# A two-layer graph network on one core: eight node tiles by counts instead of seven, and x's halves kept in DRAM

## The chip, the cores and the metric

The kernel runs on one core of one Trainium2 chip. The metric is the device time of one execution in microseconds. Before the change it is 1335.6 us, the median of three runs (1334.89 to 1339.82).

## What is computed

x has 6250 rows (nodes) of 256 values; src and dst name 100000 edges, sorted by dst. dst is 6250 times the square of a uniform number, so low nodes have many edges and high nodes few. The network adds to each node the rows of its edges' sources, twice, with two dense layers behind each sum, and the result is added to x and normalized:

```python
def gin_agg(h, src, dst, eps, n):
    agg = segment_sum(h[src], dst, num_segments=n)
    return (1.0 + eps) * h + agg
h = gin_agg(x, src, dst, eps1, n)      # 6250 x 256
h = relu(h @ W1a + b1a)                # 256 -> 512
h = relu(h @ W1b + b1b)                # 512 -> 512, this is h1
h = gin_agg(h, src, dst, eps2, n)      # 6250 x 512
h = relu(h @ W2a + b2a)                # 512 -> 512
out = layernorm(x + (h @ W2b + b2b))   # 512 -> 256
```

## The kernel before, in words

**Tiles and chunks.** Nodes are cut into 49 tiles of 128, edges into 782 chunks of 128. The sums are formed in two ways.

**Sums by gathers.** For the chunks of the higher nodes, POOL issues one indirect DMA per chunk (line 461), which fetches 128 source rows into a piece of the buffer `early` (in layer 2 also `late`). PE multiplies four such chunks with selection matrices (line 954), a second matmul puts the group's rows in their places (line 1001), and DVE adds them to the accumulators of the tiles which the group can reach (line 1011). Six pieces of four chunks can be under way; a piece's buffer comes free with its sum.

**Sums by counts.** For the lowest tiles, `HEAVY` of them, the kernel counts in layer 1 how often each source appears for each node, and multiplies these counts with all of x or h1. Counting takes one chunk after the other: DVE makes two comparison matrices (`ca`, line 1523, and `cb`, line 1532), PE multiplies them (line 1571), and DVE adds the result to the table `at` at a place that the data give (line 1594). `at` is a ring of `RING` = 4 tiles, so at most four tiles' counts are in it, and counting of further tiles waits until those of an earlier pass are cleared (line 1437). A step takes 1, 2, 4 or 8 chunks; it works from the highest heavy tile down.

**Passes of layer 1.** The heavy tiles are taken two at a time: with seven, the passes are (6,5), (4,3), (2,1) and (0). In each pass all of x goes by in 13 ranges of up to four tiles. `loading` fetches a range into `raw` (line 1188, on SP's queue), `halving` splits it into an upper half of few bits and the rest, side by side in `xh` (ACT at lines 1385 and 1392, DVE at line 1394), `factoring` turns counts into the factors `cf` (ACT, line 1415), stores them as uint16 for layer 2 (line 1423 and a DMA on ACT's queue) and has them cleared where the ring is used again, and `multiplying` forms the products (line 1457), 128x512 per node tile and source tile, so both halves in one matmul. At a pass's end `adding` puts them into the accumulators (line 1472).

**Layer 2.** h1 is read in 13 ranges from the last to the first, split in the same way (lines 1220 to 1225), the stored counts are loaded and converted (lines 1243 and 1255), and for each range and each heavy tile PE forms two products per source tile, one for each half (line 1331, 128x512). DVE collects them (line 1274). x's or h1's own rows are added as seeds (lines 866 and 883 for most tiles, 1302 and 1311 for the heavy ones of layer 2).

**Dense layers.** When a block of one or two tiles has all its parts, `dense` transposes it (line 1047), multiplies with the first weights (line 1086) and the second (line 1115), and stores h1 (line 1128) or normalizes and stores the output.

**What sets the order.** All instructions are issued in an order that a small planner works out when the program is built. It keeps a clock, costs for each operation, priorities for PE, DVE and ACT (sums by gathers first, then merges and counting, then dense work, and the products of layer 2 last), and due times for DMAs (`LOAD`, `LANDINGS`, `COUNTS` and the like). On the chip each engine and each queue then works in that fixed order. The second layer's gathers read h1 and so wait until all of it is stored.

Of the kernel before, what the change touches and what calls it, by code (L numbers as in the profile page):

```python
# [21 lines left out]
SLOTS = 32  # L22
BURST = 4
PIECES = 6
HEAVY = (7, 7)
RING = 4
W = 10
RANGE = 4
# [133 lines left out]
GATHERS = (1.28, 1.265)  # L162
LANDINGS = (5.0, 6.0)
LOAD = 6.0
SEEDS = (6.0, 12.0)
WHOLE = 16.0
COUNTS = 12.0
# [169 lines left out]
def tile_gin_residual_layernorm(  # L337
# [415 lines left out]
    def ordered(ctx):  # L753
# [4 lines left out]
        ctx.enter_context(tc.manual_schedule())  # L758

        ranges = [range(k, min(k + RANGE, NT)) for k in range(0, NT, RANGE)]  # L760
        counts = odram.tile([len(ranges), HEAVY[1], P, RANGE * P], mybir.dt.uint16, name="counts")

        def layer(number, ctx, table, width, scale, weights, ba, wide):
# [408 lines left out]
            def whole_rows(ks):  # L1172

                return min(len(ks), N // P - ks[0])
# [181 lines left out]
                    cleared[ts].more(sum(t >= RING for t in ts) * len(ranges))  # L1356

            def first_products():
                xh_room = Tiles(loan, [P, RANGE, 2, width], F32R, "xh", 2)
                raw_room = Tiles(loan, [P, RANGE, width], F32, "raw", 2)  # L1360
                ci_room = Tiles(loan, [P, RANGE * P], mybir.dt.uint16, "ci", 2)
                xh_of = {}
                turns = [(ts, r) for ts in PASSES for r in range(len(ranges))]
# [1 line left out]
                made = {(t, r): Event(plan) for ts, r in turns for t in ts}  # L1365
                factors = {}

                def loading():
                    yield ("rest", 80.0)
                    for ts, r in turns:  # L1370
                        raw = yield ("get", raw_room, 0)
                        in_rows(ranges[r], raw.tile, table)
                        token = yield ("get", xh_room, 0)
                        xh_of[ts, r] = token
                        plan.start(halving(ts, r, token.tile, raw))

                def halving(ts, r, xh, raw):
                    ks = ranges[r]
                    yield ("rest", LOAD)
                    n = whole_rows(ks)  # L1380
                    for m, js in ((P, slice(0, n)), (rows(NT - 1), slice(n, len(ks)))):
                        if js.start < js.stop:
                            c = (js.stop - js.start) * width
                            yield ("on", "ACT", act(c), 1)
                            nc.scalar.copy(xh[:m, js, 0, :], raw.tile[:m, js, :])
                            for j in range(js.start, js.stop, 2):
                                two = slice(j, min(j + 2, js.stop))
                                token = yield ("get", banks, 2)
                                c = (two.stop - j) * width
                                yield ("on", "ACT", act(c), 1)  # L1390
                                ap = bank[token.number][:m, :c].rearrange("p (k d) -> p k d", d=width)
                                nc.scalar.copy(ap, raw.tile[:m, two, :])
                                yield ("on", "DVE", dve(c), 1)
                                nc.vector.tensor_tensor(  # L1394
                                    xh[:m, two, 1, :], ap, xh[:m, two, 0, :], op=ALU.subtract
                                )
                                token.release()
                    raw.release()
                    plan.then(halved[ts, r].set)

                def factoring():
                    for ts in PASSES:
# [37 lines left out]
                def multiplying():  # L1440
                    for ts in PASSES:
# [3 lines left out]
                        for r, ks in enumerate(ranges):  # L1445
# [7 lines left out]
                            for i, t in enumerate(ts):  # L1453
# [6 lines left out]
                                        start=(k == 0), stop=(k == NT - 1),  # L1460
                                    )
                                factors[t, r].used()
                            xh_of[ts, r].release()
                        for t, token in zip(ts, tokens):
                            plan.then(plan.start, adding(t, token))

# [14 lines left out]
            def counting():  # L1481
# [1 line left out]


                F16 = mybir.dt.float16
                cb_room = Tiles(loan, [P, NT * W], F16, "cb", 10)
                ca_room = Tiles(loan, [P, BATCH, P], F16, "ca", 4)
                yield ("on", "DVE", 2.5, 4)
                si = loan.tile([P, NC], I32, tag="si", name="si")
# [399 lines left out]
```

## Time and profile before

The profiled execution took 1333.73 us, its span is 1332.0 us.

| | busy, us | instructions |
|---|---|---|
| PE, matmuls | 1171.7 | 6027 |
| PE, weight loads | 756.0 | 6027 |
| DVE | 872.8 | 2031 |
| ACT | 603.2 | 1118 |
| POOL | 963.8 | 1002 |

Of the 305.72 MB moved, 194.31 went through the queue of the gathers. Layer 1 lasts until about 676 us, when the first gather of h1 starts; layer 2 fills the rest. In the rows a line number is that of the kernel before, a name such as `early<-h,srcs` gives what is written and from what, "xN" is a count, and behind the last bar stands the idle time of the engine just before these instructions and what ended it. Busy time of PE contains the overlap of pipelined matmuls.

### The profile page before, as it was taken

Reading aid. Unit: us, or ns where it says so; the run is one execution under the profiler, and the core shown is the slowest. Engines: PE = TensorE matmul, PEld = TensorE weight load, DVE = VectorE, ACT = ScalarE, POOL = GpSimd, SP = SyncE. Lnnn points to the kernel's source line nnn. Section 1 sums busy time; section 2 is a strip of 40 time slices with the busy share of each in tenths; the row PEclk is TensorE's granted clock in tenths of the full one; section 3 lists DMA queues with packets and bytes.
Section 4 is the critical chain, followed back from the end, with each engine's and each line's share of the span. In section 5 each row is a group of like instructions: output and inputs, shape, how many; then the busy total and the mean of one; then the engine's idle time right before and its main releaser. Section 6 shows DMA issues by size and latency. Waiting matters only on the chain. (4 is left out here: it accounts for less than half of the span.)

```text
span 1332.0 us, 18717 instructions
## 1 busy us (share of the span) xinstructions
PE 1171.7 (88%) x6027; PEld 756.0 (57%) x6027; DVE 872.8 (66%) x2031; ACT 603.2 (45%) x1118; POOL 963.8 (72%) x1002
## 2 busy tenths in 40 slices
PE   2379888999899999878759899999989999999986
PEld 1145554655454655444436667767667766677755
DVE  7689888697897787323127668777756655653443
ACT  0213677767675763454255354334334433432222
POOL 6877777777777777777457677777777777777770
PEclk8589999999999999968879899999989999999999
DMA  3635666667676775566669889888889999877782
GB/s 103 189 119 178 182 219 198 207 199 227 207 225 188 219 239 170 151 211 193 198 228 333 296 268 310 252 278 287 289 271 309 301 310 301 289 244 240 242 244 69
DMA packets 160860, 305.72 MB, mean 230 GB/s; under 512 B 25672, under 2 KB 93150, under 8 KB 160754
## 3 DMA queue, kind: packets, MB, share of 16 engines
q0 software_dynamic: 63232, 194.31, 47.2%
q1 hardware_dynamic: 75110, 84.23, 19.3%
q10 hardware_dynamic: 22412, 25.89, 5.6%
q8 instruction: 51, 0.84, 0.3%
q14 instruction: 55, 0.45, 0.1%
HBM read 273.90 MB, written 30.44 MB: 228 GB/s over the span
## 5 line engine op out<-in xcount | busy, mean ns | idle before, releaser
L461 POOL DMA_INDIRECT early<-in_x_dram,srcs x494 | 488.9, 990 | 158.9 <-issue 127.4
L461 POOL DMA_INDIRECT early<-h,srcs x250 | 239.8, 959 | 101.4 <-issue 58.8
L461 POOL DMA_INDIRECT late<-h,srcs x244 | 232.5, 953 | 77.6 <-issue 60.2
L1011 DVE SCALAR_TENSOR_TENSOR acc<-bank,mask,acc 128x256 f32<-128x256 f32 (+1 forms) x368 | 212.8, 607 | 39.4 <-PE bank L1001 34.8
L1086 PE MATMUL bank<-zt,w2a_s 128*128 128x256 f32 (+2 forms) x864 | 181.8, 366 | 7.7 <-DVE acc L1011 6.5
L1115 PE MATMUL bank<-w1b_s,ht 128*128 128x512 f32 (+1 forms) x392 | 184.7, 599 | 1.1 <-DVE acc L1011 0.8
L1086 PEld LDWEIGHTS bank<-zt,w2a_s 128*128 128x128 f32 x864 | 154.8, 195 | 30.4 <-DVE acc L1011 6.9
L954 PE MATMUL bank<-early,sel 128*32 128x256 f32 (+1 forms) x1488 | 134.3, 475 | 32.7 <-DMA early<-h,srcs 15.3
L1331 PE MATMUL bank<-upper,cf 128*128 128x512 f32 (+1 forms) x343 | 149.2, 435 | 13.9 <-ACT upper L1220 13.5
L1331 PE MATMUL bank<-xr,cf 128*128 128x512 f32 (+1 forms) x343 | 138.2, 403 | 0.8 <-DVE xr L1225 0.8
L1594 DVE TENSOR_TENSOR at<-bank,at 128x490 f32 x174 | 115.9, 666 | 28.2 <-ACT cf L1415 14.7
L907 DVE TENSOR_TENSOR sel<-iota,slot 128x256 f32<-128x256 f32 (+2 forms) x116 | 50.6, 436 | 123.5 <-PE bank L954 119.5
L1086 PE MATMUL bank<-zt,w1a_s 128*128 128x256 f32 (+2 forms) x432 | 103.2, 389 | 13.7 <-ACT zt L1059 10.4
L1001 PE MATMUL bank<-split,to 128*128 128x256 f32 (+2 forms) x340 | 100.0, 415 | 15.6 <-ACT split L987 8.7
L1115 PEld LDWEIGHTS bank<-w1b_s,ht 128*128 128x128 f32 (+1 forms) x392 | 73.3, 191 | 70.8 <-issue 58.6
L1457 PE MATMUL bank<-xh,cf 128*128 128x512 f32 (+1 forms) x343 | 104.1, 440 | 8.7 <-DVE xh L1394 8.6
L1255 ACT CAST cf<-ci 128x512 fp32r<-128x512 uint16 (+1 forms) x91 | 53.8, 595 | 121.4 <-PE bank L1331 104.3
L1096 ACT ACTIVATE ht<-bank,b2a_s 128x256 f32<-128x256 f32 (+2 forms) x108 | 44.6, 451 | 139.5 <-PE bank L1086 137.0
L954 PEld LDWEIGHTS bank<-early,sel 128*32 128x32 f32 x1488 | 40.0, 112 | 113.4 <-issue 80.2
L1571 PE MATMUL bank<-cb,ca 128*128 128x490 f16 x288 | 87.6, 381 | 16.1 <-DVE at L1594 10.5
L1115 PE MATMUL bank<-w2b_s,ht 128*128 128x256 f32 (+1 forms) x392 | 101.5, 390 | 0.0
L1086 PEld LDWEIGHTS bank<-zt,w1a_s 128*128 128x128 f32 x432 | 81.9, 207 | 32.7 <-ACT zt L1059 14.9
(138 smaller groups left out, 1650.7 us busy)
## 6 DMA issues: line engine op xcount, KB each, us to landing
raw<-in_x_dram SPq DMA_DIRECT2D x48, 512.0 KB, 4.5
h<-h1r ACTq DMA_DIRECT2D x48, 256.0 KB, 2.5
xr<-h SPq DMA_DIRECT2D x12, 1024.0 KB, 7.3
counts<-ci ACTq DMA_DIRECT2D x84, 128.0 KB, 3.4
ci<-counts SPq DMA_DIRECT2D x84, 128.0 KB, 5.0
acc<-h SPq DMA_DIRECT2D x19, 512.0 KB, 7.5
early<-in_x_dram,srcs POOLq DMA_INDIRECT x494
acc<-in_x_dram SPq DMA_DIRECT2D x21, 256.0 KB, 3.9
```

The costliest lines, as they stand in the source:

```text
L461: nc.gpsimd.indirect_dma_start(out=rows_[:, j, :], out_offset=None, in_=table, in_offset=bass.IndirectOffsetOnAxis(ap=srcs[:, c : c + 1], ...
L907: nc.vector.tensor_tensor(sel[:, :n, :], iota[:, :SLOTS].unsqueeze(1).to_broadcast([P, n, SLOTS]), slot[:, c0 : c0 + n].unsqueeze(2).to_br ...
L954: mm = nc.tensor.matmul(pm[b * SLOTS : (b + 1) * SLOTS], sel[:, c - groups[g][0], :], rows_[:, l, :], start=(c == part[0]), stop=(c == par ...
L1001: nc.tensor.matmul(pu[:, i * width : (i + 1) * width], to[:used], split[:used, l, :], start=(once or l == 0), stop=(once or l == 1),)
L1011: nc.vector.scalar_tensor_tensor(acc[t], pu[:, i * width : (i + 1) * width], mask[:, t - lo[g], g : g + 1], acc[t], op0=ALU.mult, op1=ALU.add,
L1086: nc.tensor.matmul(ph[:, (f - o) * TILES * P : (f - o) * TILES * P + nb], wa[:, k, f * P : (f + 1) * P], zt[:, k, :nb], start=(k == 0), st ...
L1115: nc.tensor.matmul(po[:m], ht[:, f, i * P : i * P + m], wb[:, f, :], start=(f == 0), stop=(f == KH - 1),)
L1255: nc.scalar.copy(cf_token.tile[:, :n, :].rearrange("p k j -> p (k j)"), token.tile[:, : n * P],)
L1331: nc.tensor.matmul(bank[token.number][:, :width], cf[:m, j, :], of[:m, j, :], start=(j == 0 and of is upper), stop=(j == len(ks) - 1 and o ...
L1457: nc.tensor.matmul(bank[tokens[i].number][:, : 2 * width], cf[:m, j, :], xh[:m, j, :, :].rearrange("p a d -> p (a d)"), start=(k == 0), st ...
L1571: mm = nc.tensor.matmul(bank[token.number][:, : NT * W], a.tile[:, c % BATCH, :], b.tile, start=(j == 0), stop=(j == n - 1),)
L1594: nc.vector.tensor_tensor(to, bank[token[0].number][:, : NT * W].rearrange("p (k w) -> p k w", w=W), to, op=ALU.add,)
```

## The change

`HEAVY` becomes (8, 8): eight tiles are summed by counts in both layers, and the passes are (7,6), (5,4), (3,2) and (1,0). In layer 1 the halves of x are formed in the first pass alone; each range is then also stored to a DRAM tensor `halves` (`keeping`), and the three other passes load both halves, 1 MB per range, straight into `xh`, without `raw` and without `halving`. `xh` gets three buffers for two, `raw` one for two, and the comparison matrices `cb` eight for ten. `HALVES` is the planner's due time for these DMAs. In the first pass a buffer of `xh` comes free when its products and its store are both done.

```diff
-HEAVY = (7, 7)
+HEAVY = (8, 8)
+HALVES = 9.0
+        halves = odram.tile([len(ranges), P, RANGE, 2, D], F32, name="halves")
             def first_products():
-                xh_room = Tiles(loan, [P, RANGE, 2, width], F32R, "xh", 2)
-                raw_room = Tiles(loan, [P, RANGE, width], F32, "raw", 2)
+                xh_room = Tiles(loan, [P, RANGE, 2, width], F32R, "xh", 3)
+                raw_room = Tiles(loan, [P, RANGE, width], F32, "raw", 1)
...
+                stored = [Event(plan) for _ in ranges]
+
+                def used_rows(r):
+
+                    n, k = whole_rows(ranges[r]), len(ranges[r])
+                    whole = [(slice(0, P), slice(0, n))] if n else []
+                    return whole + ([(slice(0, rows(NT - 1)), slice(n, k))] if n < k else [])
+
                 def loading():
                     yield ("rest", 80.0)
                     for ts, r in turns:
-                        raw = yield ("get", raw_room, 0)
-                        in_rows(ranges[r], raw.tile, table)
-                        token = yield ("get", xh_room, 0)
-                        xh_of[ts, r] = token
-                        plan.start(halving(ts, r, token.tile, raw))
+                        if ts is PASSES[0]:
+                            raw = yield ("get", raw_room, 0)
+                            in_rows(ranges[r], raw.tile, table)
+                            token = yield ("get", xh_room, 0)
+                            xh_of[ts, r] = token
+                            token.users = 2
+                            plan.start(halving(ts, r, token.tile, raw))
+                        else:
+                            yield ("until", stored[r])
+                            token = yield ("get", xh_room, 0)
+                            xh_of[ts, r] = token
+                            for p, js in used_rows(r):
+                                nc.sync.dma_start(token.tile[p, js].bitcast(F32), halves[r, p, js])
+                            plan.at(plan.now + HALVES, halved[ts, r].set)
+
+                def keeping(ts, r):
+                    token = xh_of[ts, r]
+                    for p, js in used_rows(r):
+                        nc.sync.dma_start(halves[r, p, js], token.tile[p, js].bitcast(F32))
+                    yield ("rest", HALVES)
+                    token.used()
+                    yield ("rest", LOAD)
+                    stored[r].set()
...
                     plan.then(halved[ts, r].set)
+                    plan.then(plan.start, keeping(ts, r))
...
-                            xh_of[ts, r].release()
+                            (xh_of[ts, r].used if ts is PASSES[0] else xh_of[ts, r].release)()
...
-                cb_room = Tiles(loan, [P, NT * W], F16, "cb", 10)
+                cb_room = Tiles(loan, [P, NT * W], F16, "cb", 8)
```

## The prediction

> **What bounds the kernel now.** I read the page's busy line first, then the gather rows of its groups, then the timeline of POOL, then busy time by stretches.
>
> ```profile
> PE 1171.7 (88%) x6027; PEld 756.0 (57%) x6027; DVE 872.8 (66%) x2031; ACT 603.2 (45%) x1118; POOL 963.8 (72%) x1002
> ...
> L461 POOL DMA_INDIRECT early<-in_x_dram,srcs x494 | 488.9, 990 | 158.9 <-issue 127.4
> L461 POOL DMA_INDIRECT early<-h,srcs x250 | 239.8, 959 | 101.4 <-issue 58.8
> L461 POOL DMA_INDIRECT late<-h,srcs x244 | 232.5, 953 | 77.6 <-issue 60.2
> ```
> ```profile
> 8.77 1.12 POOL L461 DMA_INDIRECT early<-in_x_dram,srcs  x1 [5.50 <-DVE rawf L534]
> ...
> 650.16 0.95 POOL L461 DMA_INDIRECT early<-in_x_dram,srcs  x1 [0.30 <-issue]
> 676.63 1.13 POOL L461 DMA_INDIRECT early<-h,srcs  x1 [25.53 <-DMA h<-h1r]
> ```
>
> POOL looks 72% busy, but nearly all its idle time is "issue": a gather takes 0.95 us and 0.30 us pass before the next, so POOL can start one every 1.25 us. Layer 1's 494 gathers need 617.5 us at that pace and run from 8.77 to 651.1, 642 us: POOL is at its own pace almost throughout. It then waits 25.53 us for the last rows of h1, and layer 2 begins at 676.63. So layer 1 ends on the gathers plus a tail of 25.5 us.
>
> Layer 2, in stretches (columns: PE busy, weight loads, DVE, ACT, POOL, each with its count, then clock, DMA share, GB/s):
>
> ```profile
> 8.70:651.20 642.50, 540.52 (x2636) 308.08 (x2637) 469.78 (x1124) 342.49 (x612) 488.90 (x494) 0.92 0.63 194
> 676.60:1332.00 655.40, 611.30 (x3296) 436.81 (x3296) 395.19 (x797) 251.53 (x486) 472.30 (x494) 0.97 0.84 271
> 676.60:700.00 23.40, 13.28 (x29) 8.33 (x30) 5.49 (x11) 14.11 (x30) 17.88 (x19) 0.57 0.90 313
> 700.00:750.00 50.00, 43.53 (x218) 30.32 (x218) 35.22 (x60) 22.86 (x42) 37.59 (x40) 0.94 0.94 318
> 750.00:950.00 200.00, 198.62 (x1082) 142.55 (x1081) 155.92 (x311) 83.96 (x159) 149.69 (x157) 1.00 0.87 282
> 950.00:1000.00 50.00, 44.72 (x227) 30.81 (x226) 26.14 (x50) 17.69 (x32) 37.81 (x41) 0.93 0.85 274
> 1000.00:1200.00 200.00, 196.67 (x1077) 140.40 (x1075) 122.80 (x247) 84.60 (x156) 151.55 (x160) 1.00 0.88 293
> 1200.00:1300.00 100.00, 93.09 (x526) 67.24 (x525) 39.61 (x93) 21.64 (x48) 75.88 (x80) 0.99 0.80 241
> ```
>
> POOL keeps its 40 gathers per 50 us here too (160 in 200 us), so gathers pace layer 2 as well; but PE is close behind. Of 655.4 us PE is idle 44.1: 16.6 in the ramp to 750 (23.4 + 50 - 13.28 - 43.53), 16.9 between 750 and 1300 (550 - 533.1), and the remaining 10.6 in the tail. The question is what the one tile more costs PE there.
>
> **The change, layer 1.** From the constants of the plan: chunks by counts go from 288 to 308, so gathers go from 494 to 474 in each layer, groups from 85 to 83, counting steps (L1594) from 174 to 194. POOL loses 20 x 1.25 = 25.0 us in each layer. The other engines:
>
> ```profile
> L1594 DVE TENSOR_TENSOR at<-bank,at 128x490 f32 x174 | 115.9, 666 | 28.2 <-ACT cf L1415 14.7 <-ACT at L1437 7.4 <-PE bank L1571 1.9
> L1532 DVE TENSOR_SCALAR cb<-numbers,spot 128x490 f16<-128x490 f16 x288 | 89.4, 352 | 8.4 <-PE bank L1571 8.3
> L1571 PE MATMUL bank<-cb,ca 128*128 128x490 f16 x288 | 87.6, 381 | 16.1 <-DVE at L1594 10.5 <-DVE cb L1532 4.0 <-DVE xh L1394 1.1
> L1394 DVE TENSOR_TENSOR xh<-bank,xh 128x512 fp32r<-128x512 f32 (+1 forms) x100 | 66.8, 673 | 50.0 <-ACT bank L1392 49.5
> L1392 ACT COPY bank<-raw 128x512 f32<-128x512 f32 (+1 forms) x100 | 57.3, 580 | 20.9 <-DVE at L1594 6.8 <-DVE xh L1394 6.5 <-ACT h1r L1127 3.6
> L1385 ACT CAST xh<-raw 128x1024 fp32r<-128x1024 f32 (+1 forms) x52 | 51.6, 994 | 7.0 <-ACT ci L1423 3.3 <-PE bank L1457 1.2 <-ACT h1r L1127 1.2
> L1415 ACT CAST cf<-at 128x512 fp32r<-128x512 uint16 (+1 forms) x91 | 53.9, 592 | 43.2 <-DVE at L1594 23.3 <-ACT ci L1423 7.2 <-DVE at L1406 2.5
> ```
>
> DVE: 75 of the 100 subtractions of L1394 go (three passes of four), -75 x 0.67 = -50; 20 counting adds (13.3), 20 comparisons (7.0) and some small ones (4) come: -26 us net. ACT: 39 of L1385 and 75 of L1392 go (-38.8 - 43.0); 13 conversions of L1415, 13 copies of L1423 and 13 clearings of L1437, all of the same shape, come at 0.59 us (+23): -58 us. PE: 49 products and 20 counting matmuls come, 80 quick sums go: about +14 us, against 102 us idle in the row of layer 1. None of this is on the gathers' path unless counting becomes late (below). Fewer comparison buffers (8 for 10) can lengthen the 8.3 us for which L1532 waited for L1571; between nothing and as much again, I take nothing.
>
> DMA: x is 6.4 MB, its halves 12.8. Three raw loads go (-19.2), one store and three loads of halves come (+12.8 + 38.4), 20 gathers of 0.13 MB go, 13 count tiles of 0.13 MB come: +31 MB, spread over the some 410 us in which the passes run, so 200 GB/s becomes about 275. Layer 2 runs at 274 to 293 GB/s with POOL at full pace, so the gathers should stand it; hidden. If that cover is gone, a late landing holds PE's next sum and then POOL's buffer.
>
> The new waits sit on SP: a store of halves waits for the subtraction, and a load for a free buffer and a landed store. Behind them on SP queue the seeds of acc and the next raw load. Seeds are asked for well ahead; the raw loads, now with one buffer, are the tighter case, and only pass 1 has them.
>
> Whether the passes stay off the path is read from three places:
>
> ```profile
> 60.00:240.00 180.00, 59.17 (x89) 0.92 0.57 175
> 255.00:552.00 297.00, 56.37 (x85) 0.99 0.67 203
> ```
> ```profile
> 255.00:552.00 297.00, 58.65 (x199) 15.79 (x199) 0.99 0.67 203
> ```
> ```profile
> 255.00:552.00 297.00, 280.67 (x1427) 162.83 (x1426) 239.29 (x561) 179.92 (x321) 226.32 (x233) 0.99 0.67 203
> ```
> ```profile
> 551.66 0.67 DVE L1594 TENSOR_TENSOR at<-bank,at 128x490 f32 x1 [1.86 <-PE bank L1571]
> ...
> 631.68 0.88 DVE L1472 TENSOR_TENSOR acc<-bank,acc 128x256 f32<-128x256 f32 x2 [1.13 <-PE bank L1457]
> ```
>
> The first fence is L1594 alone: 89 steps by 240, then the ring is full and counting waits until pass 1 has been cleared, near 255. The second is L1571 in the rest: 199 chunks in 297 us, 1.49 us each, with DVE 81% and PE 94% busy (third). Counting ends at 552, and the last pass takes 80 us more, to 632. With eight tiles the ring is full after 79 steps, so 229 chunks are left at 255. At the old rate that is 341 us, ending at 596. If DVE set the rate, its 239 us become 239 - 50 + 34 = 223, at 81% 275 us, ending at 530. If PE set it, 281 + 18 = 299 at 94.5% is 316 us, ending at 571. I take 560, the middle of the ends. The last pass then needs no halving: about 13 loads of 1 MB in three buffers. The nearest row is layer 2's load of the same size:
>
> ```profile
> xr<-h SPq DMA_DIRECT2D x12, 1024.0 KB, 7.3
> ```
>
> 13/3 x (7.3 + 2 for the products) = 40 us as the lower end, the old 80 as the upper. I take 55: the last pass ends at 615, before the gathers do (651 - 25 = 626). So layer 1 gives -25. Its ends: -31, if a quarter of the 25 us comes back that the 494 gathers lost against their own pace (642 - 617.5), and, from 596 + 80 = 676 with 23 us behind it, +23.
>
> **Layer 2.** 98 products come (7 x 49 x 2 become 8 x 49 x 2). The page's group gives one a busy time of 0.43 us, but products overlap; the timeline shows what PE really pays:
>
> ```profile
> L1331 PE MATMUL bank<-upper,cf 128*128 128x512 f32 (+1 forms) x343 | 149.2, 435 | 13.9 <-ACT upper L1220 13.5
> ```
> ```profile
> 1005.57 0.39 PE L1331 MATMUL bank<-xr,cf 128*128 128x512 f32 x1
> ...
> 1006.95 0.39 PE L1331 MATMUL bank<-xr,cf 128*128 128x512 f32 x1
> 1007.18 1.08 PE L1001 MATMUL bank<-split,to 128*128 128x512 f32 x4
> ...
> 1016.92 2.78 PE L954 MATMUL bank<-late,sel 128*32 128x512 f32 x24
> 1019.64 1.13 PE L1115 MATMUL bank<-w2b_s,ht 128*128 128x256 f32 x4
> ```
>
> From 1005.57 to 1007.18 there are seven, 0.23 us from start to start, with no gap: 98 x 0.23 = +22.6. The sums of 12 gathers (24 matmuls) take 2.72, so 20 gathers fewer save 4.5; two merges of two matmuls at 0.23 save 0.9. PE's work grows by 17.2 us while POOL's shrinks by 25. POOL alone would let the layer end 25 us sooner, but PE has only 44 us idle: PE becomes the bound. The 16.9 us in the middle are waits that fall away when gathers are always ahead of PE; the ramp and the tail stay. If all of it is filled the layer's length changes by 17.2 - 16.9 = 0, if none by +17; the order is fixed when the program is built and won't fill all, so I take half: +9. ACT (13 casts, 7.7) and DVE (13 adds, 9) have 400 and 260 us free in the layer's row.
>
> **Sum.** 1333.7 (the profiled execution's own time, its span of 1332.0 and 1.7 around it) - 25 + 9 = 1317.7, so **1318**. That execution lies 1.9 under the median of the runs, 1335.6, and 1.2 under their lowest; I don't correct for it.
>
> **A rule that would read this otherwise.** The Trainium skill, "Perfetto Trace Analysis", section "Identifying the Most-Contended Engine", says that matmul busy time is no good measure of PE's headroom, and that the busy share of weight loads should be taken. By that rule PE is 67% loaded in layer 2 (436.81 of 655.4) and not the bound. The time would be that of the first rival. The rows of L1331, 0.23 us from start to start with nothing between, speak for a PE that streams without a gap, and here I follow them.
>
> **The rivals.** (1) POOL paces both layers, because PE's busy row hides room: 1333.7 - 50 = 1284. For it: POOL never drops below 40 per 50 us. Against: the gapless starts. Chance 0.12. (2) The other side: counting, not gathering, ends layer 1. The ring fills ten steps sooner, pass 1 now loads with one raw buffer and holds its halves for the store, and counting goes on at the old 1.49 us per chunk. It decides once the last pass ends later than about 632; past that a microsecond costs a microsecond. With 596 + 65 = 661, and some 23 us for the last two tiles' dense work and its landing, h1 is done at 684, +7, and layer 2's +9 goes on top: 1350. For it: PE is 94% busy just there. Against: DVE loses 50 us of halving. Chance 0.17. (3) Half of layer 1's gain is lost to crowded DMA or that chain, and layer 2 costs +12: 1333.7 - 12.5 + 12 = 1333, no change. Chance 0.13. (4) PE pays in layer 2 what the group's row says, 98 x 0.43 - 5.4 = +37: 1333.7 - 25 + 37 = 1346. For it: the row; against: the starts. Chance 0.06. (5) The change doesn't do what it says: some input's chunk reaches beyond its ten nodes and the general path runs, at a time no row here gives; the widths and margins are the same ones as before, 0.01.
>
> **How the numbers follow.** My forecast has 0.51, and its own range is 1306 to 1328. A change under 0.5% (1329 to 1342) can't be told from none. Faster: 0.12, nearly all of 0.51, and a little of rival 3, 0.64; same: most of rival 3 and the edges, 0.15; slower: rivals 2, 4 and 5 less their edges, 0.21. The range reaches from just above rival 1 to just below rival 2: 1288 to 1348.
>
> **What would show it.** Layer 1: the first gather of h near 651 instead of 676.6, after the last gather of x at 626; the last L1594 near 560, the last pass done by 632. If that pass ends later and PE or ACT waits for halves, rival 2. Layer 2: PE idle below 35 us, gathers below 40 per 50 us with POOL waiting for L954; if POOL keeps its 40 and the last 150 us are shorter, rival 1. Wrong would be above all a first pass that doesn't end by 270.

## The result and the profile after

The kernel after takes 1374.05 us (median of 4 runs, 1366.21 to 1386.56) where the kernel before took 1335.93 beside it: a ratio of 1.031, with a 95% interval of 1.027 to 1.035. It became slower; forecast were 1318 and a range of 1288 to 1348. The profiled execution took 1367.12 us, 7 under the median; its span is 1365.4. Against the profiled execution of before the first layer, counted to the first gather of h, is 14.6 us longer (691.25 for 676.63) and the second 18.8 (674.2 for 655.4).

The gathers' groups and the timeline of POOL, kernel after (busy and mean of one, then the idle time before them and what ended it; in the timeline the start, the duration and in brackets the wait):

```profile
L462 POOL DMA_INDIRECT early<-in_x_dram,srcs x474 | 475.2, 1003 | 150.5 <-issue 123.7 <-PE bank L1600 5.8 <-DVE rawf L535 5.5
L462 POOL DMA_INDIRECT early<-h,srcs x238 | 227.9, 957 | 137.4 <-DMA acc<-h 62.3 <-issue 56.7 <-DMA early<-h,srcs 5.8
```
```profile
627.99 0.95 POOL L462 DMA_INDIRECT early<-in_x_dram,srcs  x1 [0.30 <-issue]
691.25 1.03 POOL L462 DMA_INDIRECT early<-h,srcs  x1 [62.32 <-DMA acc<-h]
1296.04 0.95 POOL L462 DMA_INDIRECT late<-h,srcs  x1 [0.30 <-issue]
```

The last gather of x did come 22 us earlier, near the 25 that the count promised. But POOL then stands for 62 us instead of 25.5: layer 1 no longer ends on its gathers.

**Layer 1.** The whole layer in busy time, before and then after (PE, weight loads, DVE, ACT, POOL, each with its count, then clock, DMA share, GB/s):

```profile
8.70:676.60 667.90, 559.48 (x2729) 318.67 (x2729) 473.42 (x1132) 351.69 (x633) 488.90 (x494) 0.92 0.62 190
```
```profile
8.70:691.20 682.50, 568.98 (x2754) 326.05 (x2754) 447.76 (x1093) 296.61 (x554) 475.20 (x474) 0.95 0.70 231
```

Stretches of the kernel after; first the counting adds alone (L1623, L1594 of before), then two rows of their timeline with nothing of L1623 between them, then the waits of ACT in the last pass, then all engines:

```profile
60.00:210.00 150.00, 52.62 (x79) 0.94 0.65 208
210.00:262.00 52.00, 0.00 (x0) 1.00 0.93 323
262.00:582.00 320.00, 76.86 (x115) 0.98 0.74 243
```
```profile
204.37 1.44 DVE L1623 TENSOR_TENSOR at<-bank,at 128x490 f32 x2
267.13 0.68 DVE L1623 TENSOR_TENSOR at<-bank,at 128x490 f32 x1 [0.57 <-issue]
```
```profile
ACT ci L1452 <- DMA counts<-ci: 18.7, 7, 7.6
```
```profile
262.00:582.00 320.00, 291.16 (x1456) 164.13 (x1456) 236.51 (x567) 131.37 (x249) 244.21 (x247) 0.98 0.74 243
582.00:667.50 85.50, 73.23 (x344) 45.95 (x336) 11.38 (x26) 41.64 (x84) 35.66 (x38) 0.90 0.67 223
667.50:691.20 23.70, 11.24 (x36) 6.42 (x36) 3.55 (x10) 4.45 (x9) 0.00 (x0) 0.87 0.62 195
```

79 steps are counted by 206, then the ring is full, and the adds stand still until 267 (235 to 258 in the kernel before). The other 229 chunks take 320 us from 262 on, 1.40 each, or 1.37 from the first add on: DVE is down to 74% and ACT to 41%, but PE is at 91%. Counting ends at 582. The last pass takes 85 us more, and ACT waits in it for stores of counts to free one of the two `ci` buffers. The last two tiles' dense work and its landing take 23.7 (44 in the kernel before, from 632 to 676.6).

**Layer 2**, in its first 75 us, the stretch to the last gather and the rest; before, then after:

```profile
676.60:751.60 75.00, 58.41 (x251) 40.07 (x252) 41.26 (x71) 36.97 (x72) 55.75 (x58) 0.82 0.93 317
751.60:1301.50 549.90, 533.00 (x2911) 381.09 (x2910) 343.93 (x698) 207.89 (x395) 415.60 (x435) 0.99 0.86 277
1301.50:1332.00 30.50, 19.90 (x139) 15.65 (x137) 10.00 (x28) 6.67 (x19) 0.95 (x1) 0.94 0.17 55
```
```profile
691.20:766.20 75.00, 53.31 (x238) 35.23 (x238) 35.72 (x62) 38.77 (x72) 54.71 (x58) 0.82 0.91 312
766.20:1296.00 529.80, 515.49 (x2769) 366.45 (x2770) 342.84 (x681) 206.51 (x388) 396.49 (x416) 0.99 0.86 279
1296.00:1365.40 69.40, 59.29 (x345) 50.88 (x343) 22.23 (x59) 14.68 (x40) 0.95 (x1) 0.94 0.14 45
691.20:1365.40 674.20, 628.09 (x3350) 452.56 (x3350) 400.79 (x801) 259.95 (x500) 452.14 (x474) 0.97 0.79 259
```

The gathers need 604.8 us (75 + 529.8) for 624.9: 20 fewer, at 1.276 us each where it was 1.265. But behind the last one PE has 59.3 us of work left where it had 19.9, and the stretch grows by 38.9. The groups of that stretch show what it is, before and then after:

```profile
L1115 PE MATMUL bank<-w2b_s,ht 128*128 128x256 f32 x28 | 6.8, 383 | 0.0
```
```profile
L1117 PE MATMUL bank<-w2b_s,ht 128*128 128x256 f32 x72 | 17.6, 381 | 0.0
L1333 PE MATMUL bank<-upper,cf 128*128 128x512 f32 x16 | 6.7, 420 | 0.0
```

A tile needs eight of these matmuls (392 for 49), so nine tiles' second weights lie behind the last gather instead of three and a half, with the last products of the heavy tiles, which in the kernel before were done by 1250.

### The profile page after: what moved, and what is told of

The parts are those of the page before. It is cut to its first block, busy times and chain, and to the rows that moved or that the text cites. A ratio compares the mean times of both kernels' runs of the same rounds, so it can differ in the third digit from the quotient of the medians.

```text
span 1365.4 us, 18905 instructions
## 1 busy us (share of the span) xinstructions
PE 1197.9 (88%) x6106; PEld 779.1 (57%) x6106; DVE 852.7 (62%) x1994; ACT 556.6 (41%) x1054; POOL 929.9 (68%) x962
## 5 line engine op out<-in xcount | busy, mean ns | idle before, releaser
L462 POOL DMA_INDIRECT early<-in_x_dram,srcs x474 | 475.2, 1003 | 150.5 <-issue 123.7
L462 POOL DMA_INDIRECT early<-h,srcs x238 | 227.9, 957 | 137.4 <-DMA acc<-h 62.3
L1333 PE MATMUL bank<-upper,cf 128*128 128x512 f32 (+1 forms) x392 | 169.2, 432 | 24.5 <-ACT upper L1222 23.4
L1623 DVE TENSOR_TENSOR at<-bank,at 128x490 f32 x194 | 129.6, 668 | 62.7 <-ACT cf L1444 45.0
L1333 PE MATMUL bank<-xr,cf 128*128 128x512 f32 (+1 forms) x392 | 157.3, 401 | 0.8 <-DVE xr L1227 0.8
L1486 PE MATMUL bank<-xh,cf 128*128 128x512 f32 x392 | 117.5, 436 | 14.8 <-ACT cf L1444 14.7
L1003 PE MATMUL bank<-split,to 128*128 128x512 f32 (+2 forms) x332 | 96.9, 410 | 14.0 <-ACT split L989 8.6
L1276 DVE TENSOR_TENSOR acc<-bank,acc 128x512 f32<-128x512 f32 x96 | 64.9, 682 | 63.7 <-PE bank L1333 59.1
L1333 PEld LDWEIGHTS bank<-upper,cf 128*128 128x128 f32 (+1 forms) x392 | 75.8, 193 | 47.0 <-ACT upper L1222 24.6
L1486 PEld LDWEIGHTS bank<-xh,cf 128*128 128x128 f32 x392 | 73.3, 194 | 50.2 <-ACT cf L1444 22.7
```

The source lines that it names most:

```text
L462: nc.gpsimd.indirect_dma_start(out=rows_[:, j, :], out_offset=None, in_=table, in_offset=bass.IndirectOffsetOnAxis(ap=srcs[:, c : c + 1], ...
L1003: nc.tensor.matmul(pu[:, i * width : (i + 1) * width], to[:used], split[:used, l, :], start=(once or l == 0), stop=(once or l == 1),)
L1276: nc.vector.tensor_tensor(acc[t], bank[token.number][:, :width], acc[t], op=ALU.add)
L1333: nc.tensor.matmul(bank[token.number][:, :width], cf[:m, j, :], of[:m, j, :], start=(j == 0 and of is upper), stop=(j == len(ks) - 1 and o ...
L1486: nc.tensor.matmul(bank[tokens[i].number][:, : 2 * width], cf[:m, j, :], xh[:m, j, :, :].rearrange("p a d -> p (a d)"), start=(k == 0), st ...
L1623: nc.vector.tensor_tensor(to, bank[token[0].number][:, : NT * W].rearrange("p (k w) -> p k w", w=W), to, op=ALU.add,)
```

## The experiments

These runs went to five chips. On two of them (numbers 11 and 12) the kernel before takes 1334.5 to 1335 us, near the 1335.93 beside the result; on the other three (numbers 2, 3 and 10) it takes 1604 to 1623. They are called the faster and the slower chips here: e1 to e4 and g1 to g4 ran on the faster ones, all others on the slower. Ratios are always to the kernel before on the same chip. In the expectations theory A is rival 2 of the prediction, carried on: the counting chain and the last pass end layer 1, wherever x's halves come from; the theories beside it lay the loss on the halves' traffic and buffers (theory B) or (theory C) on how counting is dealt out to PE.

**Which part costs.** The tiles alone, the halves alone, and both with seven tiles in layer 2:

```diff
-HEAVY = (7, 7)       e1: the kernel before with
+HEAVY = (8, 8)
-HEAVY = (8, 8)       e2: the kernel after with
+HEAVY = (7, 7)
-HEAVY = (8, 8)       e3: the kernel after with
+HEAVY = (8, 7)
```

> The kernel before with eight tiles by counts, x halved anew in every pass (two xh, two raw, ten cb). Theory A, the chain of counting and passes ends layer 1, and eight tiles lengthen it whatever is done with the halves: the table is full after 79 steps instead of 89, pass 1 takes its old 120 us (ends near 258), 229 chunks at the old 1.49 us end counting near 596, the last pass of two tiles takes 85 to 100 us, 23 us follow: first gather of h near 710, 20 us later than with the halves kept; layer 2 as in the changed kernel, 674; time about 1387. Theory B, keeping the halves in DRAM (one raw buffer, stores, 1 MB loads) is what costs layer 1: first gather of h near 655, time about 1331.

> The changed kernel with seven tiles in both layers. Theory A: the full table still stops counting until pass 1 is cleared, some 15 us longer than before, but 199 chunks at 1.40 us end by 550 and the last pass has one tile and no halving, so the gathers end layer 1 as before: first gather of h at 676 to 680, layer 2 655, time 1334 to 1340. Theory B: layer 1 ends about 15 us later, as in the changed kernel: about 1350.

> The changed kernel with eight tiles by counts in layer 1 and seven in layer 2. If the 98 products that PE got in layer 2 are its whole loss there, layer 2 takes 655 us again (674 in the changed kernel) and the time is 1367 - 19 = 1348. If layer 2 is longer because of how it starts (loads and stores of layer 1 in its way), it stays near 670: 1363. Layer 1 should end near 691 as in the changed kernel.

Measured, medians: e1 1365.5 us, ratio 1.024 (1.021 to 1.026); e2 1340.45, 1.004 (1.002 to 1.006); e3 1367.45, 1.025 (1.023 to 1.028). So the tiles cost most, and the halves, which take 75 subtractions from DVE and 114 instructions from ACT, gain nothing by themselves. None of the three fell cleanly on one side of what was expected: e1 ended layer 1 at 695.4 (710 for theory A, 655 for B), e2 at 684.9 (676 to 680, or some 691), and the second layer of e3 took 664.5 (655 if the products were the whole loss, near 670 if the start was). The two layers of e1, of e2, and the second of e3 with its first 75 us:

```profile
8.70:695.40 686.70, 573.13 (x2754) 324.44 (x2754) 493.21 (x1170) 369.00 (x669) 476.42 (x475) 0.93 0.61 183
695.40:1363.00 667.60, 627.56 (x3350) 451.56 (x3350) 401.52 (x802) 259.25 (x500) 452.24 (x474) 0.97 0.80 261
```
```profile
8.70:684.90 676.20, 559.92 (x2729) 321.07 (x2729) 430.52 (x1075) 278.87 (x519) 490.01 (x495) 0.95 0.72 235
684.90:1341.20 656.30, 610.92 (x3296) 435.99 (x3296) 394.92 (x796) 251.56 (x486) 473.11 (x494) 0.97 0.84 271
```
```profile
697.20:1361.70 664.50, 614.67 (x3264) 435.62 (x3264) 394.14 (x796) 252.56 (x483) 471.46 (x494) 0.96 0.83 267
697.20:772.20 75.00, 53.35 (x232) 34.44 (x236) 37.62 (x68) 38.95 (x72) 54.67 (x57) 0.80 0.91 305
```

With eight tiles layer 1 ends at 691 to 695 whether DVE is busy 493 us (e1) or 448 (after). Layer 2 is 12 us longer in e1 too, where x's halves play no part.

In e2 layer 1 still ends on its gathers (POOL stands 20 us behind the last one), but the last one starts at 663.76 for 650.16 before: POOL waited 19.5 us for sums on PE where it had waited 7.2.

```profile
L462 POOL DMA_INDIRECT early<-in_x_dram,srcs x494 | 490.0, 992 | 171.5 <-issue 128.3 <-PE bank L956 19.5 <-DMA early<-in_x_dram,srcs 7.3
```

**The count buffers.** e4 gives the stores of counts four buffers, and takes two from `cb` for the room:

```diff
-ci_room = Tiles(loan, [P, RANGE * P], mybir.dt.uint16, "ci", 2)
+ci_room = Tiles(loan, [P, RANGE * P], mybir.dt.uint16, "ci", 4)
-cb_room = Tiles(loan, [P, NT * W], F16, "cb", 8)
+cb_room = Tiles(loan, [P, NT * W], F16, "cb", 6)
```

> The changed kernel with four ci buffers instead of two (and six cb for eight, for the room). Theory A2: each pass of two tiles is paced by the two buffers out of which the counts are stored, 26 stores at some 3.2 us; then the last pass falls from 85 us to about 55, layer 1 ends 25 to 30 us sooner (near 663), time about 1340. Rival: the loads of halves pace the last pass, which start 6.7 us apart on SP's queue: the last pass stays at 80 to 85 us and the time near 1367 or, through fewer cb, a little above.

Measured: 1370.36 us, 1.028 (1.025 to 1.031). The last pass and what is behind it, kernel e4:

```profile
590.00:656.70 66.70, 51.42 (x254) 31.86 (x254) 7.72 (x19) 34.98 (x65) 40.15 (x43) 0.90 0.77 279
656.70:691.00 34.30, 33.87 (x137) 19.44 (x135) 6.42 (x12) 11.22 (x28) 0.00 (x0) 1.00 0.50 162
```

The pass became 19 us shorter, 66.7 us instead of 85.5, though not down to the 55 that theory A expected. Yet the first gather of h came at 696. Counting ended at 590 instead of 582, PE did 22 us less in the pass (51.42 for 73.23), and after it PE worked almost without a gap for 34 us on dense work that had not been done in it. What the buffers gave was taken back by PE's dense work.

**The counting chain itself.** g1 leaves 58 of the 308 chunks uncounted (steps of more than two chunks count two), so the lowest nodes' sums lack some of their edges:

```diff
-tomake = [c + i for c, n in STEPS for i in range(n)]
+tomake = [c + i for c, n in STEPS for i in range(min(n, 2))]
```

> As f3_fewer_counts: 58 of the 308 chunks are not counted, the lowest nodes' sums lack these edges. On the slower chip the first gather of h came 22 us before that of the changed kernel beside it (816.8 against 838.9). On a chip where the kernel before takes about 1335: if counting and last pass end layer 1, the first gather of h falls from 691 to 651..665, and the ratio to before from 1.03 to about 1.005; if the gathers or the dense work end it, 683 or later.

Measured, two runs: 1351.6 us, 1.013 (1.007 to 1.019). POOL, and PE behind the last pass:

```profile
632.35 0.95 POOL L462 DMA_INDIRECT early<-in_x_dram,srcs  x1 [0.30 <-issue]
676.16 1.10 POOL L462 DMA_INDIRECT early<-h,srcs  x1 [42.86 <-issue]
```
```profile
626.00:676.20 50.20, 42.44 (x181) 23.00 (x179) 10.54 (x22) 15.14 (x33) 5.72 (x7) 0.97 0.42 135
8.70:676.20 667.50, 556.92 (x2696) 321.27 (x2696) 427.40 (x1031) 298.65 (x557) 474.04 (x475) 0.96 0.72 237
```

A miss for theory A in its simple form, which wanted 651 to 665, and no hit for the other side (683 or later). Counting ended at 539 for 582, half of the 81 us that 58 chunks at 1.40 would have given. The chain became 42 us shorter (last pass done at 626 for 667.5), the layer only 15, though the gathers, done by 633, would have let it end some 17 us sooner still (633 and the 25.5 of before; an estimate). The gap is filled by dense work: 42.4 us of PE in the 50.2 behind the pass. PE's busy time in the layer fell by 12.1 us (569.0 to 556.9), the layer by 15.

**How counting is dealt out, and the single raw buffer.** g3 counts up to four chunks per turn of PE instead of two; g4 gives the kernel after its old buffers:

```diff
-for k in range(0, len(todo), 2):           g3
+for k in range(0, len(todo), 4):
-"xh", 3) ... "raw", 1)                      g4
+"xh", 2) ... "raw", 2)
```

> As f2_turn4: up to four chunks counted per turn of PE. On the slower chip the first gather of h came 13 us earlier (825.9 against 838.9) and the time did not fall (ratio 1.017 against 1.010). Where the kernel before takes about 1335: theory C 671 to 681 for the first gather of h instead of 691; theory A 687 to 695.

> The changed kernel with two buffers of raw and two of halves, as before the change, and the rest unchanged. If the single raw buffer of the first pass is what cost layer 1 its gain: pass 1 ends some 12 us earlier (260 instead of 272), the stall of counting is 10 us shorter and the first gather of h comes 8 to 12 us earlier (680). If the rate of counting and the last pass set the end, whatever the first pass does: 687 to 695, as in the run with eight tiles and the loading of before, whose first pass ended near 246 and whose layer 1 ended at 695.

Measured, two runs each: g3 1356.71 us, 1.017 (1.007 to 1.026), first gather of h at 689.1, counting done at 579; g4 1374.94, 1.030 (1.027 to 1.034), first gather of h at 695.0. Theory C wanted the first gather of h at 671 to 681 and falls here: counting behind the stall took 1.33 us per chunk (274.5 to 579.4) instead of 1.37. So does the raw buffer: with two of them the first pass ended no earlier (its last products start at 274.1, and at 271.3 in the kernel after). g3's ratio lies below that of the kernel after, but it rests on two runs, its profiled span is only 5 us shorter, and the slower chips didn't repeat it; whether there is a small gain stays open.

**Layer 2.** g2 leaves out 85 of the eighth tile's 98 products there:

```diff
+                                    if t == 7 and (j or of is xr):
+                                        continue
```

> As f4_l2_fewer_products: 85 of the 98 products of the eighth tile in layer 2 are left out, so that tile's 128 nodes lack most of their sums. On the slower chip layer 2 did not get shorter (798.3 against 793.8). Where the kernel before takes about 1335: if PE's work sets layer 2, 674 falls to 655..660; if the start and the order of the layer set it, 666 or more.

Measured: 1376.35 us, 1.031 (1.024 to 1.039). The three stretches of its layer 2 and the layer:

```profile
694.60:769.60 75.00, 51.56 (x230) 33.46 (x230) 34.98 (x61) 38.74 (x72) 54.86 (x58) 0.82 0.92 311
769.60:1301.50 531.90, 503.49 (x2677) 353.79 (x2678) 343.24 (x682) 204.97 (x385) 396.62 (x416) 0.98 0.86 278
1301.50:1370.60 69.10, 58.95 (x360) 50.83 (x358) 22.25 (x59) 15.78 (x43) 0.95 (x1) 0.97 0.13 44
694.60:1370.60 676.00, 613.99 (x3265) 438.08 (x3265) 400.47 (x801) 259.49 (x500) 452.43 (x474) 0.96 0.79 258
```

PE does 14 us less, and the layer isn't shorter: the holes stay open (28 us idle in the middle for 14), the gathers keep their pace, and the stretch behind them is as long as before. The planner still counted these products, so the order is that of the kernel after. e3, where the planner knew of seven tiles, has 38.6 us behind its last gather instead of 69.4, with 20 gathers more ahead of it. So what PE has left at the end is laid down in the order when the program is built; here 14 us taken from PE on the chip didn't come back by themselves. Nor does this run say what PE's work costs in an order made for it.

**Moving the products up** was meant to empty that end. h1 gives the products of layer 2 the priority of the dense work, h2 does the same to the kernel before. Both ran on a slower chip:

```diff
-yield ("on", "PE", 2 * PASS * len(ks) * width, 3)
+yield ("on", "PE", 2 * PASS * len(ks) * width, 2)
```

> The changed kernel with the products of layer 2 at the same priority as the dense work instead of behind it (one number in the planner's request). In the changed kernel the last product starts at 1329, 33 us after the last gather. If the order makes the long end: the last product comes 40 us or more before the last gather, the stretch behind the last gather falls from 69 to 35..45 us, the gathers keep 1.27 us each, and layer 2 falls from 674 to 640..655; ratio to before 1.01 to 1.02. If the work of PE as a whole sets the layer: what is taken from the end comes back as waits of the gathers for sums, and layer 2 stays above 665.

> The kernel before with the same one number. Its last product starts before 1225, 75 us ahead of the last gather, and the stretch behind the last gather is 30.5 us. If the order makes the end, there is little to win here: layer 2 stays at 655 within 6 us, the ratio within 0.995 to 1.005. If moving products up holds sums of gathers back, layer 2 gets longer by more than that.

Measured: h1 1660.1 us, 1.031 (1.024 to 1.039), where the kernel after had 1.010 on another of the slower chips (f1); h2 1656.97, 1.033 (1.022 to 1.043). The stretch to the last gather and the rest, kernel after (f1) and then h1. The two are from different chips, and the profiled execution of h1 is the slowest of its five (1676.45), so only the way in which the work moves can be read from them:

```profile
838.86:1555.12 716.26, 626.58 (x2951) 413.81 (x2951) 371.62 (x730) 233.16 (x452) 454.24 (x473) 0.96 0.75 238
1555.12:1632.70 77.58, 67.46 (x400) 57.30 (x400) 27.76 (x72) 18.28 (x48) 0.95 (x1) 0.95 0.15 48
```
```profile
838.54:1582.54 744.00, 617.25 (x2911) 403.02 (x2912) 370.35 (x718) 235.32 (x447) 450.41 (x473) 0.93 0.74 229
1582.54:1674.60 92.06, 77.05 (x440) 65.79 (x440) 30.02 (x83) 20.15 (x53) 0.95 (x1) 0.93 0.14 44
```

The shorter end that was hoped for in h1 is missed: its last product starts at 1589.8, still behind the last gather, the stretch behind that gather is 92 us for 78, and the one ahead of it 28 us longer. What came true of the expectation is its other branch, that the work comes back elsewhere. In h2 the unchanged time is missed (1.033), and that moving the products up makes the kernel longer came true; no profile of the kernel before on these chips shows where.

**The slower chips.** There, f1 is the kernel after as a base and f2 to f4 are the kernels of g3, g1 and g2; e5 to e7 are the same three in an earlier batch, and e8 is e1 with seven tiles in layer 2, four `ci` buffers and four chunks per turn.

> The changed kernel, but counting asks PE for four chunks at a time instead of two (two or four steps together where they are short). Theory C: the planner gives counting one short turn on PE, with a piece of dense work between two turns, so a pair of chunks takes about 2.1 us however little work there is in it; with four per turn the 229 chunks left after the full table take some 250 us instead of 320, counting ends near 515 to 540 instead of 582, the last pass near 620, the gathers (629) end layer 1 again: first gather of h near 655, time near 1331. Rival: the work of DVE and PE itself sets the pace; then counting ends at 575 to 590 as before and the time stays near 1367.

> The changed kernel with 58 of the 308 chunks not counted (of each step of four or eight chunks only two are multiplied), so the sums of the lowest tiles are incomplete. If the chain of counting and last pass ends layer 1 (theory A), counting ends some 55 us sooner, near 525, the last pass near 610, and the gathers end layer 1: first gather of h near 655, time 1331. If something else ends it (DMA, or the dense work of the last blocks), the first gather of h stays near 691 and the time near 1365.

> The changed kernel with 85 of the 98 products of tile 7 in layer 2 left out (one of eight per range), so tile 7's sum is incomplete. If PE's load is what makes layer 2 longer, it falls by about 85 x 0.23 = 20 us, from 674 to 655, and the time to 1347. If the gathers' order or the start of the layer is behind it, layer 2 stays at 668 to 674: time 1362 to 1367.

> A candidate: the kernel before (x halved anew in every pass) with eight tiles in layer 1 and seven in layer 2, four ci buffers, and four chunks per turn. If theory C holds, counting is done by 545, each pass of two tiles takes 65 us instead of 85, layer 1 ends on its gathers near 655 and layer 2 takes 655 to 660: time 1311 to 1318. If C is wrong, layer 1 ends near 690 and the time is 1345 to 1355.

> The changed kernel itself, as the base on the same chip for the three that follow. Where the kernel before takes about 1335 us, I expect a ratio of 1.025 to 1.035 and the first gather of h at about 691 us. Where the chip is the slower one, on which the kernel before takes 1623, the run with fewer products of layer 2 has an unchanged layer 1 that ended at 843.8 and a ratio of 1.012, so I expect 1.015 to 1.03 there.

> The changed kernel with up to four chunks counted per turn of PE instead of two. Theory C (between two turns of counting the planner puts a piece of dense work, so the turn, not DVE or ACT, sets 1.40 us per chunk): the chunks behind the stall go to about 1.2 us each, counting ends some 20 us earlier and the first gather of h comes 10 to 20 us before that of the changed kernel beside it (691 becomes 671 to 681); the ratio to before falls by about 0.01. Theory A (the last pass and the dense work behind it set the end, however counting is dealt out): the first gather of h within 4 us of the changed kernel's.

> The changed kernel with 58 of the 308 chunks not counted, so the lowest nodes' sums lack these edges; all passes, gathers and products stay. If the chain of counting and last pass ends layer 1: at 1.40 us per chunk it would be 81 us shorter, until the gathers with their tail end the layer at about 628 + 23 = 651, so the first gather of h goes from 691 to 651..660 and the ratio to before falls by about 0.025. If it is the gathers or the dense work that end the layer: less than 8 us.

> The changed kernel with 85 of the 98 products of the eighth tile in layer 2 left out, so the output of that tile's 128 nodes lacks most of their sums; loads, conversions and gathers stay. If the work of PE sets layer 2: 85 x 0.23 = 19.6 us less, layer 2 falls from 674 to 655 us. If the fixed order and a slower start of the layer set it: under 8 us less, 666 or more. Layer 1 is unchanged.

| kernel | ratio, 95% interval |
|---|---|
| f1, after | 1.010 (1.003 to 1.018) |
| f2 and e5, four per turn | 1.017 (1.009 to 1.025), 1.003 (0.998 to 1.008) |
| f3 and e6, fewer counts | 0.993 (0.987 to 0.999), 0.996 (0.992 to 0.999) |
| f4 and e7, fewer products in layer 2 | 1.011 (1.006 to 1.016), 1.012 (1.003 to 1.021) |
| e8 | 1.038 (1.031 to 1.046) |

On f1 I was too high: 1.5 to 3% were expected, though its interval reaches 1.8%. The directions are those of the faster chips: fewer counts gain some 1.5%, fewer products and four per turn nothing that holds in both batches. In f2 the first gather of h did come 13 us earlier than in f1 (825.9 for 838.9), as theory C wanted, yet the time did not fall; in g3 it came 2 us earlier. e8 missed both of its times, of which the higher, 1355, would be a ratio of 1.015. The change costs 1% there instead of 3%. I rest no size on these runs, since the layers there wait for other things (last section).

## Why the prediction was wrong

Taking each layer as PE's busy time plus PE's idle time (the rows above; those of the others from the same view):

| kernel | layer 1 | busy | idle | layer 2 | busy | idle |
|---|---|---|---|---|---|---|
| before | 667.9 | 559.5 | 108.4 | 655.4 | 611.3 | 44.1 |
| after | 682.5 | 569.0 | 113.5 | 674.2 | 628.1 | 46.1 |
| e1, tiles only | 686.7 | 573.1 | 113.6 | 667.6 | 627.6 | 40.0 |
| e2, halves only | 676.2 | 559.9 | 116.3 | 656.3 | 610.9 | 45.4 |
| e3, seven in layer 2 | 688.5 | 570.1 | 118.4 | 664.5 | 614.7 | 49.8 |
| e4, four `ci` | 687.6 | 570.9 | 116.7 | 664.2 | 624.9 | 39.3 |
| g1, fewer counts | 667.5 | 556.9 | 110.6 | 670.2 | 628.6 | 41.6 |
| g2, fewer products | 685.9 | 567.1 | 118.8 | 676.0 | 614.0 | 62.0 |
| g3, four per turn | 680.4 | 569.3 | 111.1 | 671.0 | 628.1 | 42.9 |
| g4, two raw | 686.3 | 569.3 | 117.0 | 676.5 | 626.9 | 49.6 |

That busy and idle time add up to the layer shows no cause. What the table shows is that PE's idle time in layer 1 stays within 108 to 119, whatever is done to the gathers, to DVE, ACT or the counts, and in layer 2 within 39 to 50 wherever the order was made for the work. So the change, which adds 9.5 + 16.8 us to PE, lengthens the layers by 14.6 + 18.8, and the time taken from POOL appears as POOL's waiting. The table doesn't settle single layers: with the same work of PE, before and e2 differ by 8 us in layer 1, e4 and g4 by 12 in layer 2.

**The step that failed in layer 1** is "the last pass ends at 615, before the gathers do (651 - 25 = 626). So layer 1 gives -25". It ended at 667.5, nearly 39 us behind the last gather (629), and 23.7 us of dense work and landing followed: counting was done 22 us later than I took (582 for 560), and the pass took 85.5 us for 55. Under it lies "about +14 us, against 102 us idle in the row of layer 1. None of this is on the gathers' path unless counting becomes late (below)". The 102 us were taken as free room. Most of the idle time of the kernel after lies where it did not help counting, as its stretches show:

```profile
8.70:60.00 51.30, 19.38 (x78) 8.35 (x78) 37.86 (x148) 8.23 (x13) 40.86 (x35) 0.90 0.55 165
60.00:210.00 150.00, 124.03 (x609) 70.67 (x610) 133.48 (x294) 72.22 (x130) 114.96 (x116) 0.94 0.65 208
400.00:582.00 182.00, 170.28 (x857) 93.90 (x857) 142.46 (x352) 60.33 (x113) 139.15 (x141) 0.99 0.67 217
```

32 of the 113.5 lie ahead of 60, where DVE prepares the indices, 26 between 60 and 210, and 12 + 12.5 in the last pass and behind it; where the rest is counted, from 262 to 582, PE is at 91 to 94%. That another order could not use these gaps is not shown.

**Counting and the last pass.** Of the three ends that I had worked out (530 by DVE, 571 by PE, 596 at the old rate) I took 560, the middle. Measured was 582. The one by PE came nearest: its 316 us of counting, behind a start of 262 for 255, against 320. That is in part luck: PE did 291 us of work there for the 299 reckoned, at 91% for 94.5. The end by DVE rests on a wrong sum. It takes all 75 subtractions out of the 239 us between 255 and 552, but only 54 of the 100 (36.1 us) lie there; with them 239 - 36 + 34 is 237, and measured are 236.5. The 30 chunks more ate in this stretch what the halving had cost. The last pass, which I took as 55 us from its loads, was mis-sized by a term that I left out: it now has two tiles, so 26 conversions and stores of counts through two `ci` buffers, not only 13 loads. It took 85.5, and 66.7 with four buffers, where also 22 us of PE's dense work had moved out of it. The 23 us behind it were right (23.7). So rival 2, with 684 for layer 1, named what happened, with 0.17; 691.25 is 7 beyond it. Its reading is only half the cause, though. When the chain was shortened by 42 us the layer gained 15, because PE still had the dense work to do.

**What the change took and gave** was as worked out: DVE in layer 1 473.42 to 447.76 (-25.7, forecast -26), ACT 351.69 to 296.61 (-55, forecast -58), PE +9.5 (+14), and in layer 1 some 31 MB more (231 GB/s over 682.5 us for 190 over 667.9), as forecast. The crowding did no harm to the gathers of this kernel, which still waited mostly for their own issue (123.7 of 150.5). The test that I had named, a first pass that ends by 270, was missed by 2 us, and it was the wrong sign to watch: in e1 that pass was done by 246 and counting went on at 250, but at 1.47 us per chunk instead of 1.37, and it ended at 587, 5 us later than with the halves kept.

**The step that failed in layer 2** is "the order is fixed when the program is built and won't fill all, so I take half: +9". PE's work was right (+16.8), the gathers' gain nearly (20.1 us of the 25), but nothing of the idle time was filled: 46.1 for 44.1. The middle has 14.3 idle for 16.9, the start loses 5.1. There PE's first product waits for ACT, which has the seeds of h ahead of it in its queue:

```profile
692.12 2.38 ACT L885 ACTIVATE acc<-acc,e 128x1024 f32<-128x1024 f32 x2 [9.80 <-DMA acc<-h]
696.56 0.80 PE L1333 MATMUL bank<-upper,cf 106*128 106x512 f32 x1 [15.68 <-ACT upper L1222]
```

In the kernel before that wait was 6.11 us. The order of e1 has no such loss (58.8 us of PE in the first 75, as before) and its layer is still 12 us longer; e3 has the loss (53.4) without the products, and is 9 longer. The two make up the 18.8 about, the larger part coming with the products. How much of that part is PE's work and how much its place behind the last gather isn't separated.

**The other rivals.** Rival 1 fell: POOL paces layer 2 only up to its last gather. With it falls the reading by the Trainium skill, "Perfetto Trace Analysis", section "Identifying the Most-Contended Engine": weight loads are again 67% (452.56 of 674.2), which by that section leaves room on PE, while 16.8 us more work went with a layer that is 18.8 longer. Rival 3 fell with layer 1, which lost 14.6 us where half of the gain was to stay. Rival 4's dearer products are refuted by PE's row: +16.8, not +37.

What stays open: whether PE's work alone holds layer 1 at its length, since g1 took work from DVE and length from the chain as well; what layer 2 would take in an order that leaves PE less behind the last gather; and why the start of layer 2 is late in some orders.

## What to carry to other kernels

An engine's idle time counts as room only in the stretch where the added work must run: sum it by stretch, and take away what lies ahead of the first data and behind the last. When two engines are as near to each other as POOL and PE were here, taking work from one and giving it to the other can show the price on the second and no gain on the first. With an order fixed when the program is built, look at how much work the order leaves behind the last transfer; here that stretch swallowed the whole gain of the gathers.

## What the runs showed of the hardware that was not expected

The kernel before takes a fifth longer on three of the five chips: 1604 to 1623 us for 1335. The kernel after on one of these (f1), its gathers of x and its layer 1:

```profile
L462 POOL DMA_INDIRECT early<-in_x_dram,srcs x474 | 475.9, 1004 | 291.9 <-issue 124.7 <-PE bank L956 95.7 <-PE bank L1600 25.0
8.70:838.90 830.20, 610.39 (x2754) 341.73 (x2754) 453.63 (x1095) 297.75 (x554) 475.90 (x475) 0.86 0.59 190
```

A gather costs POOL the same 1.00 us, and DVE is as busy as on the faster chips (453.6 for 447.8). But PE is idle for 220 us of the layer instead of 113.5 and busy for 610.4 instead of 569.0 with the same 2754 matmuls, and POOL waits 96 us for its sums. Of PE's waits in this layer 48 us are put down to nothing that the profile shows ("issue"); in the kernel after on the faster chip none are. What makes PE late there was not found.

A store of 128 KB could hold its buffer long: ACT waited up to 7.6 us for one in the last pass, while 223 GB/s were moved, less than the 323 of the stretch from 210 to 262. With four buffers (e4) it waited 2.4 at most, at 279 GB/s.
